# Two of four attention heads' results transposed by 16-bit DMA transposes, and their on-chip places rearranged

## The chip, the cores and the metric

One NeuronCore of a Trainium2 chip runs the whole kernel. The metric is the device time of one execution in microseconds (us), and the time of a kernel is the median of its runs. About 0.2% (some 7 us) is what a measurement of this kernel can tell from no change.

## What is computed

The input is 32 graphs of 512 nodes with 512 features each, and a 512 x 512 adjacency for each. Two pre-normed attention layers follow one another. The reference, cut to what matters here:

```python
h = relu(layernorm(x)); x = x + L0(h, adj)          # one head, attention over the nodes, no projection
h = relu(layernorm(x)); x = x + L1(adj, h)

def gat_layer(x, mask, W, a_src, a_dst, bias, concat):   # L1 calls it twice
    xl = (x @ W).reshape(B, N, H, F)
    asrc = einsum('bnhf,hf->bnh', xl, a_src);  adst = einsum('bnhf,hf->bnh', xl, a_dst)
    e = leaky_relu(asrc[:, :, None, :] + adst[:, None, :, :], 0.2)
    attn = softmax(where(mask[..., None], e, -1e9), axis=1)
    out = einsum('bsdh,bshf->bdhf', attn, xl)
    return (concat over heads, or mean) + bias
# in L1:
h = elu(gat_layer(x, mask, W1, ..., concat=True))    # H = 4 heads of F = 256
h = gat_layer(h, mask, W2, ..., concat=False)        # one head, 1024 -> 512
```

The place of the change is the elu between the two calls of `gat_layer`: the output of each head is 512 nodes x 256 features with the nodes on the partitions, and the product with W2 contracts over the features, so that it needs them on the partitions. Each head's result is therefore transposed.

## The kernel before

The sizes are T = 4 node tiles of P = 128 nodes, KD = 4 blocks of 128 features, H = 4 heads. Everything is float32 but the masks, which are bf16.

**Order of the work.** The function `tile_preln_gat_kernel` (L261) doesn't emit instructions in the order in which it is written. It hands each one to `Plan.op` (L59) as a closure, with the engines that may run it, a cost for each, and the parts of buffers that it reads and writes. `Plan.run` (L87) then drafts a schedule up to six times: a list scheduler (L131) simulates five engines, a chain of transfers (L140, L210 to 215: one at a time, at most eight in flight) and the places of each kind of buffer (`slots`, L317), ranks the work by its latest start and emits the best draft. So the order on each engine, which place a buffer gets, and which of two engines runs an eviction are decided at build time by these costs. On the chip each engine runs its own list strictly in that order.

**One graph**, in the loop at L985: `masks1` and `layer1_project` (W1), `layer2_out` of the graph before, the four heads (`layer1_scores`, then `layer1_head`), `layer0_out` and `layer1_in` of the next graph, `layer0_scores` of the one after, and `layer2_project` (W2). The plan mixes these, so that TensorE has matmuls of neighbouring graphs to run while a chain of another waits.

- `edge_weights` (L583) makes one head's 512 x 512 weights `E`: rows of scores go through DRAM and come back broadcast over the partitions (`in_lines` L548, `row_of` L565, into a `row` place), a largest value is taken (L592), then per tile a leaky relu (L613, ACT), a subtraction (L616, DVE), the mask (L618, POOL) and an exponential (L621, ACT).
- `aggregate` (L624) multiplies `E` by the head's values: for each node tile four matmuls, L631. Each is two TensorE instructions in the trace. Its first matmul also takes the place of the result, so TensorE can't begin before that place is free.
- `layer1_head` (L887) divides by the row's sum and adds the bias (L894, L897, DVE) into `v`, a place of [128, 4, 256] for the whole head; then for each half of the node tiles an exponential of v - 1 (L906, ACT, into the one place `e`) and min/max (L909, DVE). The bias has been raised by 1 at the start (L419), so that `v` holds elu + 1. Eight TensorE transposes (L921, recorded at L485) turn the head over, feature block by feature block, into two PSUM banks; `evict` (L514) takes each bank to `h1T` on ACT (L520) or DVE (L526), subtracting the 1.
- `layer2_project` (L930) multiplies by W2 with `products` (L774), a seven-product scheme on quarters (node half i, contraction half j). Its matmuls are L826, its sums of quarters L807 (DVE) and L808 (POOL); `h1T[0]` (heads 0 and 1) and `h1T[1]` (heads 2 and 3) are the two contraction halves.
- The masks are transposed by DMA already: `transposed_mask` (L669) issues four transfers of [128, 512] bf16 per mask from the SP queue (L673). SP also issues the loads and stores of `x` (L660, L762, L770, L964).

The places that matter here:

```python
        "v": places("v", 2, [P, T, F]),
        "e": places("e", 1, [P, T // 2, F]),
        "row": places("row", 2, [P, N]),
```

All three hold 2 KB per partition in 512 values, `v` twice that.

Of the kernel before, what the change touches and what calls it, by code (L numbers as in the profile page):

```python
# [9 lines left out]
F32 = mybir.dt.float32  # L10
BF16 = mybir.dt.bfloat16
AF = mybir.ActivationFunctionType
ALU = mybir.AluOpType
PSUM = bass.MemoryType.PSUM

P = 128
# [26 lines left out]
class Plan:  # L43
# [87 lines left out]
    def draft(self, rank):  # L131
# [7 lines left out]
        now = {e: [] for e in names}  # L139
        lock, moving, landed = {"DVE": 0.0, "POOL": 0.0}, 0.0, []  # L140
        vacant = {kind: [(0.0, k) for k in range(len(s))] for kind, s in self.slots.items()}
# [22 lines left out]
        while len(draft.order) < len(ops):  # L164
# [42 lines left out]
            if locks and e in lock:  # L207
                at = max(at, lock["POOL" if e == "DVE" else "DVE"])
                lock[e] = at + occupied
            for held in moves:  # L210
                if len(landed) >= self.IN_FLIGHT:
                    at = max(at, landed[-self.IN_FLIGHT])
                moving = max(moving, at) + held
                there += moving - at
                landed.append(at + there)
# [39 lines left out]
def by_dma(n, after=2000.0):  # L255

    return 350.0, after, n / 300.0


@with_exitstack  # L260
def kernel(  # L261
# [51 lines left out]
    def places(kind, n, shape, dtype=F32, pool=big):  # L313
# [14 lines left out]
        "E_one": places("E_one", 2, [P, T, N]),  # L328
        "v": places("v", 2, [P, T, F]),
        "e": places("e", 1, [P, T // 2, F]),  # L330
        "col": places("col", 12, [P, T]),
        "ac": places("ac", 4, [P, 4, T]),
        "row": places("row", 2, [P, N]),
        "r": places("r", 8, [P, 1]),
# [16 lines left out]
    minus_half = const.tile([P, T], F32, name="minus_half")  # L351
    nc.vector.memset(minus_half, -0.5)
    minus_one = const.tile([P, 1], F32, name="minus_one")
    nc.vector.memset(minus_one, -1.0)
# [25 lines left out]
    AHEAD, LATER = 400, 300  # L380
    NEAR0, NEAR2, FAR = False, False, ()

# [3 lines left out]
    def load_constants():  # L386
# [12 lines left out]
        for k in range(KD):  # L399
            for half, q in enumerate(QUARTER[k // (KD // 2)]):  # L400
# [3 lines left out]
                )  # L404
        fetch(HF, lambda: b1_r, rows(b1, HF), W["b1"](1), -LATER)
        fetch(D, lambda: b2_r, rows(b2, D), W["b2"](0), -LATER)
# [4 lines left out]
        for i in range(2):  # L411
# [5 lines left out]

        op(
            "DVE", on_dve(HF), lambda: nc.vector.tensor_scalar(b1_r, b1_r, 1.0, None, op0=ALU.add), W["b1"](1), W["b1"](0),  # L419
            -LATER,  # L420
        )
        return att
# [91 lines left out]
    def evict(src, dst, src_of, dst_of, n, bias=None, psum_half=False):  # L514
# [13 lines left out]
        op(("ACT", "DVE"), (on_act(n, bias is not None), on_dve(n)), (by_act, by_dve), src, dst)  # L528

    def spread(part, col_of, ahead):  # L530

        row = Buffer("acc")
        for t in range(T):
            pe_transpose(
                ahead, row, lambda t=t: row.at[:, node_block(t)], part, lambda t=t: col_of(t).to_broadcast([P, P]), ident, t
            )
        return row
# [7 lines left out]
    def first(ac, n):  # L545
        return lambda: ac.at[:, :n, :].rearrange("p n t -> p (n t)")

    def in_lines(cols_of, part, n):  # L548

        pt, flat_, lines = Buffer("acc"), Buffer("e"), Buffer("lines")  # L550
        m = n * T
        op(
            "PE", on_pe(P, transpose=True),
            lambda: nc.tensor.transpose(pt.at[:m, :P], cols_of(), ident),  # L554
            part + flat_("place"), pt(0), AHEAD,
        )
        evict(pt(0), flat_(0), lambda: pt.at[:m, :P], lambda: flat_.at[:m, 0, :P], P)
        op(
            "SP", by_dma(4 * m * P, 3000.0),
            lambda: nc.sync.dma_start(lines.at[:n].rearrange("n (t p) -> (n t) p", p=P), flat_.at[:m, 0, :P]),  # L560
            flat_(0), lines(0), AHEAD,
        )
        return lines
# [105 lines left out]
    def transposed_mask(m, mT):  # L669
        for t in range(T):  # L670
            op(
                "SP", (2200.0, 3000.0, 600.0),
                lambda t=t: nc.sync.dma_start(mT.at[:, :, node_block(t)], m.at[:, t, :], transpose=True),  # L673
                m(t), mT(t),
            )
# [36 lines left out]
    def layer0_scores(b):  # L712
# [16 lines left out]

        L0[b] = (h0, edge_weights("E_one", scores, ac, in_lines(first(ac, 2), scores, 2) if b else None, 0, m0, m0T, not b or NEAR0))  # L730

# [5 lines left out]
    def layer1_in(b):  # L737
# [5 lines left out]
        for k in range(KD):  # L743
            pt = Buffer("acc")
            for t in range(T):
                pe_transpose(
                    AHEAD, pt, lambda t=t, pt=pt: pt.at[:, node_block(t)], hn(t) + hT("place"),
                    lambda t=t, k=k: hn.at[:, t, node_block(k)], ident, t,
                )
            evict(pt(*ROW), hT((k, 0), (k, 1)), lambda pt=pt: pt.at, lambda k=k: hT.at[:, k, :], N)  # L750
        HT[b] = hT
# [104 lines left out]
    def layer1_project(b):  # L856
# [8 lines left out]
        def dst(i, j, r, c):  # L865
# [4 lines left out]
            lambda i, j: hT.at[:, j * nk : (j + 1) * nk, i * HN : (i + 1) * HN],  # L870
            lambda i, j, g: hT(*((j * nk + 2 * g + k, i) for k in range(2))),
            nk, weights_of("w1", KINDS_1), W1, range(H // 2), lambda w, k, c: w1_s[w][:, k, c, :], dst, xl,
        )

    def layer1_scores(b, h):
# [8 lines left out]
        ac, lines = AC[b]  # L884
        return edge_weights("E", ac(0), ac, lines, 2 * j, m1T, m1, h not in FAR)

    def layer1_head(b, h, E):  # L887

        xl, j = L1[b][h // 2], h % 2
        v = Buffer("v")  # L890
        for t in range(T):
            acc = aggregate(E, t, xl, lambda s: ((j, s),), lambda s: xl_of(xl)[:, s, j, 2:], F + 1, v)
            r = Buffer("r")
            op("DVE", on_dve(8), lambda acc=acc, r=r: nc.vector.reciprocal(r.at, acc.at[:, F : F + 1]), acc(0) + xl(2), r(0))  # L894
            op(
                "DVE", on_dve(F, 1.0, True),
                lambda t=t, acc=acc, r=r: nc.vector.scalar_tensor_tensor(  # L897
                    v.at[:, t, :], acc.at[:, :F], r.at, b1_r[:, h * F : (h + 1) * F], op0=ALU.mult, op1=ALU.add
                ),
                acc(0) + r(0) + W["b1"](0), v(t),  # L900
            )
        for half in range(2):
            ts = slice(half * T // 2, (half + 1) * T // 2)
            parts = v(*range(T)[ts])
            e = Buffer("e")
            op("ACT", on_act(2 * F, 1), lambda e=e, ts=ts: nc.scalar.activation(e.at, v.at[:, ts, :], AF.Exp, bias=minus_one), parts, e(0))  # L906
            op(
                "DVE", on_dve(2 * F),
                lambda e=e, ts=ts: nc.vector.scalar_tensor_tensor(  # L909
                    v.at[:, ts, :], e.at, 1.0, v.at[:, ts, :], op0=ALU.min, op1=ALU.max  # L910
                ),
                parts + e(0), parts, lock=True,
            )
# [3 lines left out]
        nk = F // P  # L917
        for k in range(nk):
            pt = Buffer("acc")
            for t in range(T):  # L920
                pe_transpose(  # L921
                    0, pt, lambda t=t, pt=pt: pt.at[:, node_block(t)], v(t) + h1T("place"), lambda t=t, k=k: v.at[:, t, node_block(k)], ident, t
                )
# [6 lines left out]
    def layer2_project(b):  # L930
# [19 lines left out]
        )  # L950
        L2[b] = (edge_weights("E_one", ac(0), ac, in_lines(first(ac, 2), ac(0), 2) if b < B - 1 else None, 0, m1T, m1, b == B - 1 or NEAR2), xl)

# [84 lines left out]
```

## Time and profile before

| | before |
|---|---|
| median of 3 runs | 3676.41 us (3674.74 to 3678.61) |
| profiled execution: its own time | 3677.66 us |
| its span, first to last instruction | 3675.7 us |
| TensorE (PE) busy | 3598.6 us, 98%, 17620 matmul instructions |
| weight loads (PEld) busy | 3118.9 us, 85% |
| VectorE (DVE) busy | 2953.4 us, 80% |
| ScalarE (ACT) busy | 1873.2 us, 51% |
| GpSimd (POOL) busy | 1456.5 us, 40% |
| DMA | mean 89 GB/s; the SP queue's packets took 26.9% of 16 engines' span |
| granted TensorE clock | 0.994 of full speed |

Engine names are PE, DVE, ACT, POOL and SP; a name with q is the sequencer, and a group such as "L621 ACT ACTIVATE E<-E 128x512" is all instructions of that line, engine, operation and shape, with count, summed busy time and mean duration. Matmuls overlap in the pipeline, so the duration of one is longer than the distance between two starts. A transfer has two times: how long SP is held by issuing it, and how long after that it lands.

### The profile page before, as it was taken

How to read it: one execution, taken by the hardware profiler on the slowest of the kernel's cores; microseconds unless marked ns; L12 is line 12 of the kernel's file. 1: busy time of each engine (PE TensorE's matmuls, PEld its weight loads, DVE VectorE, ACT ScalarE, POOL GpSimd, SP SyncE). 2: the span in 40 equal slices, each digit the busy share in tenths (PEclk: the TensorE clock that was granted, in tenths of full speed). 3: DMA queues.
4: the chain of work that ended last, by engine and by line, in shares of the span. 5: the costliest groups of instructions: out<-in, count | busy, mean ns of one | idle time of the engine just before them, and what ended most of it. 6: DMA issues, size and time to landing. Idle time of an engine off the chain costs nothing.

```text
span 3675.7 us, 51476 instructions
## 1 busy us (share of the span) xinstructions
PE 3598.6 (98%) x17620; PEld 3118.9 (85%) x17620; DVE 2953.4 (80%) x7487; ACT 1873.2 (51%) x3426; POOL 1456.5 (40%) x1269
## 2 busy tenths in 40 slices
PE   5799999999999999999999999999999999999999
PEld 4688888888888888888888888888888888888877
DVE  7888778877788887788777888877887877887755
ACT  2455455555455555555555555554555545555543
POOL 3534334433334343344343344333443433443322
PEclk9899999999999999999999999999999999999999
DMA  6234333343333343323333323433233433333220
GB/s 166 58 92 109 76 90 85 79 109 89 91 85 89 86 110 84 88 82 87 98 99 83 88 89 81 110 87 92 81 92 87 109 78 90 85 82 106 86 65 32
DMA packets 313767, 328.54 MB, mean 89 GB/s; under 512 B 151736, under 2 KB 190368, under 8 KB 313504
## 3 DMA queue, kind: packets, MB, share of 16 engines
q1 hardware_dynamic: 279712, 291.70, 26.9%
q0 software_dynamic: 33792, 33.56, 6.4%
q8 instruction: 138, 2.26, 0.2%
q14 instruction: 125, 1.02, 0.1%
HBM read 257.16 MB, written 68.01 MB: 88 GB/s over the span
## 4 chain that ended last, share of the span: by engine, by line
PE 95%; DVE 2%; ACT 0%; POOL 0%; issue 0%; DVEq 0%
PE acc L631 47%; PE acc L826 42%; PE acc L485 6%; PE acc L554 1%; DVE junk L592 1%; DVE E L616 0%; DVE x L649 0%; DVE E_one L616 0%; DVE st L491 0%; ACT E_one L621 0%; DVE v L897 0%; DVE w L457 0%; POOL E L618 0%; POOL E_one L618 0%; DVE junk L375 0%
## 5 line engine op out<-in xcount | busy, mean ns | idle before, releaser
L631 PE MATMUL acc<-pair,E 128*128 128x257 f32 x4096 | 950.2, 381 | 5.5 <-ACT E L621 5.5
L618 POOL TENSOR_TENSOR E<-E,m 128x512 f32<-128x512 f32 x512 | 596.6, 1189 | 769.6 <-DVE E L616 527.5
L631 PEld LDWEIGHTS acc<-pair,E 128*128 128x128 f32 x4096 | 760.0, 190 | 110.1 <-ACT E L621 7.1
L826 PE MATMUL acc<-w_T,E 128*128 128x257 f32 (+1 forms) x2048 | 517.9, 380 | 0.0
L631 PE MATMUL acc<-h,E_one 128*128 128x256 f32 (+1 forms) x2048 | 479.7, 381 | 4.8 <-ACT E_one L621 4.8
L592 DVE CUSTOM_DVE_ANT_0 junk<-m1T,acc 128x512 bf16<-128x512 bf16 x640 | 436.2, 682 | 29.1 <-ACT acc L580 16.5
L631 PE MATMUL acc<-xl,E_one 128*128 128x257 f32 x1984 | 459.6, 379 | 0.0
L621 ACT ACTIVATE E<-E 128x512 f32<-128x512 f32 x512 | 317.0, 625 | 272.3 <-POOL E L618 266.5
L826 PEld LDWEIGHTS acc<-w_T,E 128*128 128x128 f32 x2048 | 383.4, 190 | 61.5 <-DVE E L807 0.2
L631 PEld LDWEIGHTS acc<-h,E_one 128*128 128x128 f32 x2048 | 381.8, 190 | 61.3 <-ACT E_one L621 5.8
L631 PEld LDWEIGHTS acc<-xl,E_one 128*128 128x128 f32 x1984 | 370.5, 189 | 50.8 <-ACT E_one L621 0.7
L839 DVE TENSOR_TENSOR pair<-acc,pair 128x258 f32<-128x258 f32 (+1 forms) x390 | 164.6, 424 | 300.6 <-PE acc L826 261.1
L613 ACT ACTIVATE E<-row,ac 128x512 f32<-128x512 f32 x512 | 343.7, 708 | 80.9 <-PE acc L631 78.1
L518 ACT COPY pair<-acc 128x258 f32<-128x258 f32 (+1 forms) x486 | 181.4, 374 | 380.2 <-PE acc L826 376.1
L906 ACT ACTIVATE e<-v,minus_one 128x512 f32<-128x512 f32 x256 | 184.8, 722 | 317.8 <-DVE v L897 221.8
L616 DVE TENSOR_TENSOR E<-E,acc 128x512 f32<-128x512 f32 x512 | 324.5, 674 | 3.4 <-PE acc L485 3.2
L618 POOL TENSOR_TENSOR E_one<-E_one,m0T 128x512 f32<-128x512 f32 x128 | 144.8, 1155 | 335.9 <-DVE E_one L616 335.8
L826 PE MATMUL acc<-w,hT 128*128 128x258 f32 x1024 | 268.1, 381 | 0.0
L826 PE MATMUL acc<-w,E 128*128 128x257 f32 (+1 forms) x1024 | 267.6, 381 | 0.0
L909 DVE SCALAR_TENSOR_TENSOR v<-e,v 128x512 f32<-128x512 f32 x256 | 225.6, 881 | 44.0 <-ACT e L906 42.3
L667 POOL DMA_DIRECT2D m<-in_adj_dram x64 | 51.5, 805 | 502.2 <-DVE col L592 465.9
L649 DVE SCALAR_TENSOR_TENSOR x<-acc,r,x 128x256 f32<-128x256 f32 x512 | 239.3, 478 | 13.6 <-PE acc L631 7.3
(108 smaller groups left out, 5899.7 us busy)
## 6 DMA issues: line engine op xcount, KB each, us to landing
row<-lines SPq DMA_DIRECT2D x442, 256.0 KB, 3.5
x<-in_x_dram SPq DMA_DIRECT2D x32, 1024.0 KB
m<-in_adj_dram POOLq DMA_DIRECT2D x64, 512.0 KB, 5.8
spill<-x SPq DMA_DIRECT2D x32, 1024.0 KB, 4.4
x<-spill SPq DMA_DIRECT2D x32, 1024.0 KB, 5.5
out_dram<-x SPq DMA_DIRECT2D x30, 1024.0 KB
m0T<-m SPq DMA_TRANSPOSE x128, 2.5
m1T<-m SPq DMA_TRANSPOSE x128, 2.8
```

The source lines that it names most:

```text
L485: op("PE", on_pe(P, transpose=True), lambda: nc.tensor.transpose(dst_of(), src_of(), identity), src, dst(part), ahead)
L518: nc.scalar.copy(dst_of(), src_of())
L592: lambda t=t: nc.vector.tensor_tensor_reduce(junk, mask_max.at[:, t, :], a_row.at, 1.0, LOWEST, ALU.add, ALU.max, accum_out=amax.at[:, t : ...
L613: lambda t=t: nc.scalar.activation(E.at[:, t, :], c_row.at, AF.Prelu, bias=a_of(t), scale=1.0, alpha=SLOPE),
L616: op("DVE", on_dve(N), lambda t=t: nc.vector.tensor_sub(E.at[:, t, :], E.at[:, t, :], m_row.at), m_row(*ROW) + E(t), E(t))
L618: "POOL", on_pool(N, True), lambda t=t: nc.gpsimd.tensor_add(E.at[:, t, :], E.at[:, t, :], mask.at[:, t, :]),
L621: op("ACT", on_act(N), lambda t=t: nc.scalar.activation(E.at[:, t, :], E.at[:, t, :], AF.Exp), E(t), E(t))
L631: lambda s=s: nc.tensor.matmul(acc.at[:, :n], E.at[:, s, node_block(t)], of(s), start=(s == 0), stop=(s == T - 1)),
L649: lambda acc=acc, r=r, f=f, t=t: nc.vector.scalar_tensor_tensor(X.at[:, t, f], acc.at[:, :HD], r.at, X.at[:, t, f], op0=ALU.mult, op1=ALU. ...
L826: lambda k=k: nc.tensor.matmul(acc.at[:, :width], at[a]()[:, k, node_block(r)], weight_of(w, k, c), start=(first and k == 0), stop=(k == n ...
L906: op("ACT", on_act(2 * F, 1), lambda e=e, ts=ts: nc.scalar.activation(e.at, v.at[:, ts, :], AF.Exp, bias=minus_one), parts, e(0))
L909: lambda e=e, ts=ts: nc.vector.scalar_tensor_tensor(v.at[:, ts, :], e.at, 1.0, v.at[:, ts, :], op0=ALU.min, op1=ALU.max),
```

## The change

In heads 0 and 1 (`TURNED`), the TensorE transposes and the PSUM evictions go. Instead, for each half (two node tiles, 512 float32 values per partition): the elu itself is formed, as max(v, -relu(1 - exp(v))), in two ACT instructions and one on DVE; ACT copies it, seen as 1024 16-bit values, into a `row` place with low and high halves separated; SP issues one transposing DMA of [128, 1024] 16-bit values, eight blocks of 128 x 128, back into the `v` place; and ACT copies from there into `h1T`, interleaving the halves again. Heads 2 and 3 keep the TensorE transposes.

`v` becomes four places of half a head, and the kind `e` is given up: there are three `row` places, which rows of scores, flat lines (`in_lines`), exponentials and the separated halves share. The 1 is added to the bias of heads 2 and 3 only. The planner charges a transposing transfer with its own two-part cost (`by_turning`) and now follows ordinary transfers and transposes in two chained queues. The rest of the diff (finer parts of `hT`; flags that were constant written out) doesn't alter what is run.

```diff
-        lock, moving, landed = {"DVE": 0.0, "POOL": 0.0}, 0.0, []
+        lock, taken, landed = {"DVE": 0.0, "POOL": 0.0}, [0.0, 0.0], []
...
-            for held in moves:
+            if moves:
                 if len(landed) >= self.IN_FLIGHT:
                     at = max(at, landed[-self.IN_FLIGHT])
-                moving = max(moving, at) + held
-                there += moving - at
+                for k, held in enumerate(moves):
+                    taken[k] = max(taken[: k + 1] + [at]) + held
+                there += taken[len(moves) - 1] - at
                 landed.append(at + there)
...
+def by_turning(n):
+    return 1100.0 + n / 1000.0, 800.0, n / 300.0, 1400.0 + n / 180.0
...
-        "v": places("v", 2, [P, T, F]),
-        "e": places("e", 1, [P, T // 2, F]),
+        "v": places("v", 4, [P, 2, F]),
...
-        "row": places("row", 2, [P, N]),
+        "row": places("row", 3, [P, N]),
...
+    TURNED = (0, 1)
...
+    def turned(values_of, src, place, results_of, dst):
+        e = Buffer("row")
+        op(
+            "ACT", (1040.0, 1100.0),
+            lambda: nc.scalar.copy(
+                e.at.bitcast(U16).rearrange("p (b f) -> p b f", b=2), values_of().bitcast(U16).rearrange("p (f b) -> p b f", b=2)
+            ),
+            src + place, e(0),
+        )
+        op(
+            "SP", by_turning(4 * P * N),
+            lambda: nc.sync.dma_start(
+                values_of().bitcast(U16).rearrange("p (c n) -> p c n", n=P), e.at.bitcast(U16), transpose=True
+            ),
+            e(0), src,
+        )
+        def pair():
+            out = results_of()
+            k, t = out.shape[1], out.shape[2]
+            nc.scalar.copy(
+                out.bitcast(U16).rearrange("p k t (n b) -> p k t n b", b=2),
+                values_of().bitcast(U16).rearrange("p (b t k n) -> p k t n b", b=2, k=k, t=t),
+            )
+        op("ACT", (1160.0, 1220.0), pair, src, dst)
...
-                "SP", (2200.0, 3000.0, 600.0),
+                "SP", by_turning(2 * P * N),
...
-        v = Buffer("v")
+        vs = [Buffer("v"), Buffer("v")]
         for t in range(T):
+            v, i = vs[2 * t // T], t % (T // 2)
...
+        for half in range(2):
+            v, e = vs[half], Buffer("row")
+            parts = v(*range(T // 2))
+            values = lambda v=v: v.at.rearrange("p t f -> p (t f)")
+            if h in TURNED:
+                op("ACT", on_act(2 * F), lambda e=e, values=values: nc.scalar.activation(e.at, values(), AF.Exp), parts, e(0))
+                op(
+                    "ACT", on_act(2 * F, 1),
+                    lambda e=e: nc.scalar.activation(e.at, e.at, AF.Relu, bias=one, scale=-1.0), e(0), e(0),
+                )
+                op(
+                    "DVE", on_dve(2 * F),
+                    lambda e=e, values=values: nc.vector.scalar_tensor_tensor(
+                        values(), e.at, -1.0, values(), op0=ALU.mult, op1=ALU.max
+                    ),
+                    parts + e(0), parts, lock=True,
+                )
+                turned(
+                    values, parts, h1T("place"),
+                    lambda half=half: h1T_of(h1T)[:, j * nk : (j + 1) * nk, half * HN : (half + 1) * HN].rearrange(
+                        "p k (t n) -> p k t n", n=P
+                    ),
+                    h1T(*((j * nk + k, half) for k in range(nk))),
+                )
+                continue
...
-        for k in range(nk):
+        for k in () if h in TURNED else range(nk):
             pt = Buffer("acc")
```

## The prediction, made before the result was known

> **What bounds the kernel now.** I read the page's busy times first, then PE's waits, then the PE timeline of one graph.
>
> ```profile
> PE 3598.6 (98%) x17620; PEld 3118.9 (85%) x17620; DVE 2953.4 (80%) x7487; ACT 1873.2 (51%) x3426; POOL 1456.5 (40%) x1269
> ...
> PE 95%; DVE 2%; ACT 0%; POOL 0%; issue 0%; DVEq 0%
> ```
>
> The second line is the chain that ended last: 95% of the span is PE behind PE. A busy PE alone would not prove a full one, so here are PE's waits between 160 and 3520 us, and the busy times of 500 us in the middle.
>
> ```profile
> PE acc L485 <- DVE v L909: 1.3, 1, 1.3
> PE acc L485 <- DVE col L599: 0.7, 1, 0.7
> PE acc L631 <- ACT E_one L621: 0.3, 1, 0.3
> ...
> 1500.00:2000.00 500.00, 500.00 (x2458) 433.93 (x2458) 403.44 (x1017) 257.63 (x477) 195.19 (x172) 1.00 0.33 90
> ```
>
> In 3360 us PE waits 2.3 us. Everything else is hidden, and a PE instruction removed there is gained whole unless a new wait appears. How much one is worth is seen in the PE timeline (start, length, count):
>
> ```profile
> 1505.02 1.47 PE L826 MATMUL acc<-w,pair 128*128 128x257 f32 x6
> 1506.33 1.90 PE L826 MATMUL acc<-w_T,E 128*128 128x257 f32 x8
> 1508.07 1.90 PE L826 MATMUL acc<-w,pair 128*128 128x257 f32 x8
> ...
> 1613.81 0.60 PE L485 MATMUL acc<-ident,v 128*128 128x128 f32 x4
> 1614.25 1.89 PE L631 MATMUL acc<-h,E_one 128*128 128x256 f32 x8
> ```
>
> Eight matmuls take 1508.07 - 1506.33 = 1.74 us, 0.2175 each; four transposes take 1614.25 - 1613.81 = 0.44 us, 0.109 each. One graph repeats every 111.83 us (the same long L826 piece of the chain stands at 396.01 and 507.85). Pricing all PE instructions so gives 3587 us, and PE's idle 77 us lie almost wholly in the first 130 us (the constants, on DVE) and the last 200.
>
> **What the Trainium skill says.** (1) "TensorE: Matmul & The Clock Gate", Part 4, gives about 275 ns for a transpose in a kernel. The trace's mean is 273, but that is one's length in the pipeline; the distance, 109 ns, is what a removed one gives back. The measurement decides. (2) "DMA: Bandwidth & Descriptors", DMA Transpose (X-bar), takes 2-byte types only, so float32 must be split into halves and joined again. The mask transposes, bf16, agree. It also forbids two transposing streams at once; here all are SP's, so no wait is added. (3) The same page, HWDGE ordering, says an engine consumes descriptors in ring order: a transpose issued behind a 1 MB load on SP's queue stands behind its data. No row shows the two together. (4) "ScalarE: Activation LUTs", What ACT_TABLE_LOAD costs: 186 ns + 0.833 ns an element, 93 more for a pointer bias, back-to-back overlapping by 93. The trace agrees within a few per cent: 587 ns for the copy L580 of 512 (613 by the page), and in ACT's timeline an L613 starts 0.51 us after a 0.58 us L580.
>
> **The change, part by part.** The rows that give durations:
>
> ```profile
> L906 ACT ACTIVATE e<-v,minus_one 128x512 f32<-128x512 f32 x256 | 184.8, 722 | 317.8 <-DVE v L897 221.8 <-DVE r L894 94.6 <-issue 1.2
> ...
> L485 PE MATMUL acc<-ident,v 128*128 128x128 f32 x1024 | 153.7, 273 | 2.7 <-DVE v L909 2.7
> ...
> L520 ACT ACTIVATE pair<-acc,minus_one 128x512 f32<-128x512 f32 x161 | 105.9, 678 | 98.9 <-PE acc L485 98.9
> ...
> L526 DVE TENSOR_SCALAR pair<-acc 128x512 f32<-128x512 f32 x95 | 64.6, 680 | 7.4 <-PE acc L485 7.4
> ...
> L673 SPq DMA_TRANSPOSE m1T<-m x128: 1188/1201/2461, 82.8 to 3567.0; - x128
> ...
> DMA to landing us min/median/max: 2.4/2.5/4.2
> ```
>
> *Removed on PE.* Of the 1024 transposes of `v`, 512 go: 16 a graph. 16 x 0.109 = 1.74 us a graph, x 32 = **-55.7 us**, all on the path.
>
> *Other engines, from the order of the changed program.* ACT gains 128 relus of about 0.70 (as L520), 128 separating and 128 joining copies of 1024 elements; it loses 96 L520 (0.68), 29 hT (0.59) and 147 projection evictions (0.37), and half its L906 become plain exponentials (0.72 to 0.63). The copies are new: 587 + 512 x 0.833 = 1.01 us from L580, 1.04 by the page. Below, 0.6 if 16-bit values went at double pace; above, 2.0 if the strided 2-byte side halved it. I take 1.04. Sum +90 + 266 - 137 - 12 = +207 us: ACT at about 2080 of 3622, 57%. DVE gives up 32 L526 (22 us) and 55 sums of quarters (70) and takes the evictions that ACT lost (82): about level, 81%. POOL takes the sums, +83 us, 43%. None is a bound; the free time of ACT and DVE hides it. The bias split and the finer `hT` parts cost nothing measurable; they hide behind the start's loads.
>
> *The transfers.* Per graph four transposes of 256 KB. The nearest row is the masks' 128 KB: 1.2 us on SP, then 2.5 to land. With twice the blocks it is at least the same and at most twice: 1.2 to 2.4 on SP, 2.5 to 5.0 landing; I take 1.6 and 3.7. SP gets 4 x 1.6 = 6.4 us a graph, and in the new order they stand behind the store of `out` and the load of `x`, ahead of the spill (L762) and load-back (L770), which wait for later work anyway. While two mask transposes are issued back to back (1559 to 1562.5 us) DMA is 0.54 busy, so four of twice the size at that rate (4 x 2.5 x 0.54 = 5.4 us of 110) add some 5% of the DMA's time.
>
> *The added wait.* A `v` place is taken by the first matmul of `aggregate`, so TensorE itself waits for it, with all PE work queued behind. Heads 2 and 3 take the places that heads 0 and 1 leave after the joining copy. In the new PE order, from the last matmul of a half of head 0 to the first that takes its place again, there are 14.3 to 15.2 us of PE work at the cadences above. One half's own chain: 1.1 (reciprocal, two L897) + 0.63 + 0.70 + 0.88 (L909) + 1.04 + 1.6 + 3.7 + 1.04 = 10.7 us, some 0.4 more for signals. That leaves 3 us, but ACT is in order: between the first half's exponential and its joining copy stand 16 other ACT instructions (7 exponentials of `E` or `v`, 7 relus and leaky relus, 2 copies). At the distances of ACT's timeline, 0.53, 0.61 and 0.95, and with the exponential and the joining copy themselves, they come to 11.5 us; begun 1.0 after the last matmul, they end at 12.5. So ACT, not the chain, sets the margin: 1.8 us on the tightest place. The transfer has 6.6 us between the separating and the joining copy. With my values (5.3) it fits; with the upper ends (7.4) it is 0.8 late, inside the margin; behind a 1 MB load still moving (spill<-x lands in 4.4) it can be later. The second consumer, W2, has more room: 23 us of PE work from head 1's last matmul to the first L826.
>
> *Shared rows.* Three places serve what two `row` and one `e` served, with 4 more short holders a graph. A late row stops ACT (L580 waited 36.3 us for rows in all), which has 43% spare; I cost it at nothing, at most 0.3 us a graph if that cover goes.
>
> *Ends.* In the first and last graph PE has no spare matmuls to put into these chains: I allow 4 us, between -5 and +12. For occasional misses of the tight place I allow 0.1 us a graph, 3 us; bounds 0 to 3.4 a graph (below). Sum against the profiled execution: 3677.7 - 55.7 + 4 + 3 = 3629.0. The median of runs lies 1.3 lower: **3628 us**.
>
> **The rivals.**
>
> *A. Part of the gain is lost at the places.* If the 16-bit copies take their upper end, 2.0 us, the three in ACT's stretch add 2.9 us, 1.1 more than the margin, and PE waits that much a graph: 3676.4 - 55.7 + 4 + 32 x 1.1 = 3660. For it speaks how little margin there is; against it, that ACT's durations in the trace follow the number of elements, and that PE's waits for all places together are 2.3 us before.
>
> *B. Slower: the transposes land behind the load of `x`.* SP's order puts the store of `out` and the 1 MB load just ahead of the first of the four. If the ring makes it wait for the load's 4.4 us, and it takes 2.4 + 5.0 itself, the joining copy comes 11.8 us after the separating one where 6.6 are covered: 5.2 late, less the margin of 1.8, and PE stands 3.4 us at the place, while ACT holds the exponentials of head 3 behind the joining copy. It decides from 1.74 us of wait a graph, a transfer of 10.1 us. At 3.4: 3676.4 + 32 x (3.4 - 1.74) + 4 = 3733 us. Against it: only the first of the four can meet the load, and the load takes its full time only if it starts as late.
>
> *C. The change doesn't give the PE time back, since another engine takes over.* DVE at 81% is nearest; between 500 and 3500 us it had 18% free with PE waiting for it 2 us. It would have to wait on POOL and ACT at the wrong times, 1.74 us a graph: no change, 3676. The shares speak against it.
>
> **Chances.** Forecast (3612 to 3640) 0.62; A (3640 to 3669) 0.15; C or about level (3669 to 3684) 0.06; B (above) 0.17. Faster by over 0.2% 0.77, within 0.2% 0.06 (0.2% is about what a measurement of this kernel can tell from no change), slower 0.17. The range runs from the full gain with better ends, 3612, through A to level, 3676; B is left out.
>
> **What would show it.** Right: 17108 PE instructions, a graph every 110.1 us, PE's waits in the middle still a few us; the new SP row near 1.6 with landing near 3.7; the two ACT copies near 1.04; ACT near 57%. Rival A or B: PE acc (the L631 of before) waits for ACT's joining copy in most graphs, and that copy waits for the DMA of `v` (B) or not (A). I am wrong if the transfers land in over 5 us, if the copies cost over 1.3 us, or if PE waits for rows.

## The result, and the profile after

The changed kernel takes **3658.15 us** (median of 5 runs, 3656.49 to 3661.75), the kernel before 3677.87 on the same chip: a ratio of 0.995, 95% interval 0.9936 to 0.9965. That is faster by 19.7 us, where 48 were forecast. The time lies inside the range, but under half of the predicted gain came.

First the page of the changed kernel: the engines' busy times, and the chain that ended last.

```profile
PE 3557.8 (97%) x17108; PEld 3059.5 (84%) x17108; DVE 2966.4 (81%) x7521; ACT 2075.1 (57%) x3595; POOL 1560.7 (43%) x1324
...
PE 78%; DVE 11%; POOL 2%; DMA 2%; ACT 2%; issue 1%; SPq 1%; DVEq 0%; ACTq 0%; POOLq 0%
```

The first line is what the prediction asked for: 17108 PE instructions, ACT at 57%, DVE at 81%, POOL at 43%. The second line is not. Before, 95% of the chain was PE behind PE; now DVE holds 11%. So PE stands somewhere. Here are PE's waits between 160 and 3500 us of the changed kernel (total us, times, longest), and then 500 us in the middle:

```profile
PE acc L497 <- DVE col L641: 16.2, 27, 1.5
PE acc L673 <- ACT E_one L663: 1.8, 5, 0.6
PE acc L868 <- DVE pair L881: 0.9, 1, 0.9
```

```profile
1500.00:2000.00 500.00, 497.52 (x2404) 428.72 (x2403) 406.86 (x1022) 286.81 (x505) 217.82 (x185) 1.00 0.39 101
```

PE was busy in every one of these 500 us before, and is idle for 2.5 of them now. None of the waits is for a place of `v` or for a joining copy, which rivals A and B and most of the prediction were about. PE waits for `col`, a head's maxima: L641 (L599 before) is a DVE instruction on 128x4 values, and L497 with `ident,col` is the spread that lays them along a row. The lines are those of the changed kernel from here on.

The new instructions themselves, from the groups of the changed kernel, and the view of the transposing transfer's line (durations in ns, min/median/max; then issue to landing in us):

```profile
L565 ACT COPY pair<-v 128x1024 uint16<-128x1024 uint16 x128 | 147.3, 1150 | 0.6 <-DMA v<-row 0.6
L549 ACT COPY row<-v 128x1024 uint16<-128x1024 uint16 x128 | 132.5, 1035 | 12.2 <-DVE v L962 9.1 <-issue 1.2
```

```profile
L556 SPq DMA_TRANSPOSE v<-row x128: 1232/1232/1516, 133.0 to 3595.0; - x128
...
DMA to landing us min/median/max: 2.7/2.7/2.7
```

The separating copy (L549) took 1.035 us and the joining one (L565) 1.150, where 1.04 was taken for each; the issue held SP for 1.23 us (1.6 taken). The 2.7 us run from the start of the issue to landing, so SP's time is part of them. The view knows the landing of only 15 of the 128 transfers. By the trace's completion records, of which some are missing, the median of all 128 is 2.7 us as well, but 14 took 4 us or more (at most 5.8), and ten of these were issued 2 to 3.3 us after the load of `x`. Only once in the kernel did a joining copy wait for its transfer (SP's issue, then ACT's copy):

```profile
1253.59 1.23 SPq L556 DMA_TRANSPOSE v<-row  x1
1258.84 1.16 ACT L565 COPY pair<-v 128x1024 uint16<-128x1024 uint16 x1 [0.57 <-DMA v<-row]
```

This transfer took 5.2 us, cost ACT 0.57 us, and no wait of PE names it.

**What one stand looks like.** Three timelines of the changed kernel around 1558 us (start, length; in brackets the idle time before it and its releaser), PE, DVE, then POOL:

```profile
1555.54 2.76 PE L673 MATMUL acc<-xl,E_one 128*128 128x257 f32 x12
1559.50 0.65 PE L497 MATMUL acc<-ident,col 128*128 128x128 f32 x4 [1.20 <-DVE col L641]
```

```profile
1558.11 0.15 DVE L639 TENSOR_TENSOR col<-ac,col 128x4 f32<-128x4 f32 x1
1558.18 0.48 DVE L691 SCALAR_TENSOR_TENSOR x<-acc,r,x 128x256 f32<-128x256 f32 x1
1558.58 0.87 DVE L641 SCALAR_TENSOR_TENSOR col<-col 128x4 f32<-128x4 f32 x1
1559.37 0.15 DVE L685 RECIPROCAL r<-acc 128x1 f32<-128x1 f32 x1
```

```profile
1558.27 1.16 POOL L660 TENSOR_TENSOR E_one<-E_one,m 128x512 f32<-128x512 f32 x1 [1.65 <-DVE col L639]
```

L641 has four elements a partition; its sister L639 takes 0.15 us. Here it takes 0.87, and ends at 1559.45, 0.02 after GpSimd's addition of the mask does (1558.27 + 1.16 = 1559.43). PE starts 0.05 later. Of the 1.20 us that PE waits here, the collision makes 0.72; the rest is a chain that was late already. The pattern holds throughout: in the changed kernel 21 of the 192 L641 and 20 of the 192 L639 took over 0.3 us, and each of these 41 ended 16 to 24 ns after a GpSimd instruction did.

The larger L691 reads one of its two big inputs from PSUM; GpSimd starts 0.09 us into it, and neither is stretched. All of this is what the Trainium skill describes on "SBUF — State Buffer", Who interferes with whom (and above it, SBUF: two separate sides): DVE and GpSimd share one pair of ports as an exclusive lock; a DVE instruction with two SBUF inputs and a GpSimd instruction that reads SBUF don't share it, the later one waits for the whole of the earlier. The kernel's planner knows that rule (`lock=True` on an operation), but the two 128x4 operations L639 and L641 don't carry the mark.

**Collisions alone are not new.** In the kernel before the same instruction (L599 there) was stretched as well, as its mean in the groups of before shows:

```profile
L599 DVE SCALAR_TENSOR_TENSOR col<-col 128x4 f32<-128x4 f32 x192 | 48.9, 255 | 3.0
```

255 ns there, 229 in the changed kernel. In the kernel before, PE had other work queued ahead of the spread (0.7 us of waits for `col` in all); in the changed order, the spread stands next. So the theory to test has two halves: the collision, and an order in which nothing covers it.

### The profile page after: what moved, and what is told of

Its sections match the earlier page's. It is cut to its first block, busy times and chain, and to the rows that moved or that the text cites. A ratio compares the mean times of both kernels' runs of the same rounds, so it can differ in the third digit from the quotient of the medians.

```text
span 3656.0 us, 51114 instructions
## 1 busy us (share of the span) xinstructions
PE 3557.8 (97%) x17108; PEld 3059.5 (84%) x17108; DVE 2966.4 (81%) x7521; ACT 2075.1 (57%) x3595; POOL 1560.7 (43%) x1324
## 4 chain that ended last, share of the span: by engine, by line
PE 78%; DVE 11%; POOL 2%; DMA 2%; ACT 2%; issue 1%; SPq 1%; DVEq 0%; ACTq 0%; POOLq 0%
PE acc L673 37%; PE acc L868 36%; PE acc L497 4%; DVE junk L634 4%; POOL E_one L660 2%; DVE E_one L658 2%; DVE x L691 1%; DVE E L658 1%; DMA row<-lines 1%; SPq L715 1%; DMA m0T<-m 1%; DVE pair L881 0%; ACT E L655 0%; PE acc L596 0%; DVE col L639 0%
## 5 line engine op out<-in xcount | busy, mean ns | idle before, releaser
L673 PE MATMUL acc<-pair,E 128*128 128x257 f32 x4096 | 924.4, 380 | 4.6 <-ACT E L663 4.6
L660 POOL TENSOR_TENSOR E<-E,m 128x512 f32<-128x512 f32 x512 | 618.6, 1238 | 344.7 <-DVE E L658 312.8
L673 PE MATMUL acc<-h,E_one 128*128 128x257 f32 (+1 forms) x2048 | 497.2, 382 | 8.6 <-ACT E_one L663 4.8
L655 ACT ACTIVATE E<-row,ac 128x512 f32<-128x512 f32 x512 | 334.6, 708 | 12.6 <-DMA row<-lines 12.3
L658 DVE TENSOR_TENSOR E<-E,acc 128x512 f32<-128x512 f32 x512 | 332.4, 674 | 2.9 <-PE acc L497 2.1
L530 ACT COPY pair<-acc 128x258 f32<-128x258 f32 (+1 forms) x339 | 126.5, 374 | 309.4 <-PE acc L868 307.3
L530 ACT COPY xl<-acc 128x257 f32<-128x257 f32 x219 | 82.0, 374 | 345.9 <-PE acc L868 345.7
L941 DVE SCALAR_TENSOR_TENSOR v<-acc,r,b_r 128x256 f32<-128x256 f32 x512 | 242.5, 478 | 8.5 <-DVE r L938 0.7
L868 PE MATMUL acc<-w,pair 128*128 128x257 f32 x1024 | 244.3, 379 | 0.0
```

The source lines that it names most:

```text
L530: nc.scalar.copy(dst_of(), src_of())
L655: lambda t=t: nc.scalar.activation(E.at[:, t, :], c_row.at, AF.Prelu, bias=a_of(t), scale=1.0, alpha=SLOPE),
L658: op("DVE", on_dve(N), lambda t=t: nc.vector.tensor_sub(E.at[:, t, :], E.at[:, t, :], m_row.at), m_row(*ROW) + E(t), E(t))
L660: "POOL", on_pool(N, True), lambda t=t: nc.gpsimd.tensor_add(E.at[:, t, :], E.at[:, t, :], mask.at[:, t, :]),
L673: lambda s=s: nc.tensor.matmul(acc.at[:, :n], E.at[:, s, node_block(t)], of(s), start=(s == 0), stop=(s == T - 1)),
L868: lambda k=k: nc.tensor.matmul(acc.at[:, :width], at[a]()[:, k, node_block(r)], weight_of(w, k, c), start=(first and k == 0), stop=(k == n ...
```

## The measure used below

PE's idle time in the trace understates the loss, because short pauses lie inside modelled durations. I added up, from 500 to 3020 us of PE's timeline, the distance between the starts of successive pieces less what their count should take (0.109 us a transpose, 0.2172 a matmul), and took off the same sum of the kernel before, which holds the artefacts of cutting the timeline. Divided by the 22.5 graphs of that stretch it is the **stand per graph**: 26.1 / 22.5 = 1.16 us in the changed kernel. A time follows: 3677.5, less 55.7 where the 512 transposes are gone, plus 32 stands. The changed kernel: 3677.5 - 55.7 + 37.1 = 3659, measured 3658.

| kernel | PE instructions | stand per graph, us | worked out, us | measured, us |
|---|---|---|---|---|
| before | 17620 | 0 (reference) | 3677 | 3677 |
| changed | 17108 | 1.16 | 3659 | 3658 |
| none_turned | 17620 | 2.89 | 3770 | 3764 |
| masks_old_price | 17108 | 0.52 | 3638 | 3646 |
| before_unturned | 17108 | 0.05 | 3623 | 3629 |
| small_locked | 17108 | -0.03 | 3621 | 3626 |
| one_input | 17108 | 0.49 | 3637 | 3639 |
| none_one_input | 17620 | 0.71 | 3700 | 3690 |
| signal_61 | 17108 | 1.60 | 3673 | 3672 |
| before_prices | 17620 | 0.46 | 3692 | 3689 |
| none_locked | 17620 | 1.57 | 3728 | 3727 |
| before_locked | 17620 | 0.81 | 3703 | 3704 |
| before_places | 17620 | 0.51 | 3694 | 3692 |
| all_locked | 17108 | 0.15 | 3627 | 3629 |

Two numbers a kernel, its PE work and its stand, give every time within 11 us, eight of the thirteen within about 3. Nothing is needed for the transfers, the copies or ACT's extra work. The sum says how long PE stood, not why; that is what the experiments are for. A second reading agrees within 0.2 us a graph for every kernel: the distance from one graph to the next in the trace (first transposes of `h`, mean over 21 graphs), 111.83 us before and 111.27 in the changed kernel.

## The experiments

The theories: **collision**, as above. **Prices**: the planner's new prices for the mask transposes make a worse order. **Lost cover**: the removed transposes had covered waits that now show. **Turned path**: the copies and transfers themselves hold something up. **Re-planning**: any change of the plan moves the time so much, with no one cause.

### none_turned: the changed kernel with no head turned

```diff
-    TURNED = (0, 1)
+    TURNED = ()
```

> The changed kernel with no head turned by transfers (TURNED empty): its planner and its places, but all four heads transposed on TensorE. Prices theory (the mask transposes' new, lower price on SP took slack out of the plan, and TensorE now stands at the spread of a head's maxima behind late score rows): the loss of about 1.1 us a graph is there without any turning, 3677 + 35 = 3712 us, with TensorE waiting for DVE's maxima in most graphs. Turned-path theory (the copies and transfers of the turned heads disturb ACT, SP and DVE): like the kernel before, 3677 us. Lost-cover theory (1.74 us less TensorE work a graph leaves the score chain uncovered): 3677 us too.

Measured 3763.92 us, ratio 1.0234 (1.0219 to 1.0249): far above every theory. PE's waits of this kernel:

```profile
PE acc L497 <- DVE col L641: 40.5, 60, 1.4
PE acc L497 <- DVE v L981: 13.1, 14, 1.0
```

The same wait, two and a half times as large, in a kernel without a single turned head. So the loss doesn't need the copies and transfers, and in the changed kernel no wait of PE names them: the turned path falls. Measured against this kernel, turning gains 106 us, almost twice the PE work that it removes; that is the difference of two orders, not a price of turning.

### masks_old_price: the mask transposes planned at their old price

```diff
-                "SP", by_turning(2 * P * N),
+                "SP", (2200.0, 3000.0, 600.0),
```

> The changed kernel with one edit: the mask transposes are planned at their old price (2.2 us on SP, 3.0 after, 0.6 moving) in place of the new one. Nothing else is edited; the plan's order changes. Prices theory: the waits for DVE's maxima go, 3658 - 33 = 3625 us. Turned-path and lost-cover theories: unchanged within some 8 us, 3650 to 3666 us.

Measured 3645.76 us, 0.9914 (0.9899 to 0.9929): between the two expectations. The waits for `col` are gone, but in their place PE waits for `v` of DVE (4.5 us, 16 times). The price matters through the order it makes, but the old price doesn't bring the rest of the gain.

### before_unturned: the PE work alone

The kernel before, with heads 0 and 1 not transposed at all: the copy to `h1T` takes `v` as it lies. It leaves out these two heads' transposition.

```diff
+            if h < 2:
+                evict(
+                    v(*ROW) + h1T("place"), h1T((j * nk + k, 0), (j * nk + k, 1)), lambda k=k: v.at[:, :, node_block(k)],
...
+                )
+                continue
```

> The kernel before, with the transposes of heads 0 and 1 left out and nothing in their place: the evictions copy the untransposed values from v to the same place (so the output of layer 1 is computed from untransposed values in these two heads). Its planner, prices and places are those of before. It shows what the removed TensorE work is worth with no turned path at all. Prices theory and turned-path theory: the whole 55.7 us, 3620 to 3625 us, no waits in the middle. Lost-cover theory: the score chain is uncovered here too, 3650 us or more.

Measured 3628.91 us, 0.9869 (0.9855 to 0.9884): 48.5 us, of the 55.7 that the removed transposes were priced at, and 4 us above the expectation. PE is full in its middle (busy in all of the 500 us from 1500), and the 3650 or more that lost cover asked for is far off: lost cover falls. A graph repeats here every 110.26 us, where the full gain would give 110.09, so by estimate some 5 of the missing 7 us are pauses too short to show as waits.

### small_locked: the two small operations marked for the planner

```diff
-        op("DVE", on_dve(T), lambda: nc.vector.tensor_add(z.at, ac.at[:, k + 1, :], amax.at), scores + amax(*ROW), z(0))
+        op("DVE", on_dve(T), lambda: nc.vector.tensor_add(z.at, ac.at[:, k + 1, :], amax.at), scores + amax(*ROW), z(0), lock=True)
...
-            z(0), m(0),
+            z(0), m(0), lock=True,
```

> The changed kernel with one edit: the two small DVE instructions between a head's maxima and their spread are planned apart from GpSimd's work (lock), as one of them took 0.87 us beside GpSimd where 0.15 is usual. Contention theory (that instruction is what TensorE waits for): most of the waits go, 3635 us. Prices theory: its 0.7 us is only part of a late chain; 3645 to 3658 us. Others: 3658 us.

Measured **3626.29 us**, 0.9861 (0.9845 to 0.9878): the fastest kernel of the study, 31.9 us under the changed one. Its waits of PE and a stretch of its middle:

```profile
PE acc L868 <- DVE pair L881: 0.5, 1, 0.5
PE acc L673 <- DVE E L658: 0.4, 1, 0.4
PE acc L673 <- DVE x L691: 0.2, 1, 0.2
```

```profile
1500.00:2000.00 500.00, 500.00 (x2420) 433.77 (x2419) 413.00 (x1045) 291.92 (x520) 212.52 (x186) 1.00 0.41 104
```

PE is full again. But how? The small operations are still stretched in this kernel:

```profile
L641 DVE SCALAR_TENSOR_TENSOR col<-col 128x4 f32<-128x4 f32 x192 | 56.8, 296 | 0.1
```

296 ns, more than the 229 of the changed kernel (its sister L639 194, against 221). The mark did not take the collisions away; it gave an order in which PE has something else to do. This run can't tell a cured collision from a lucky new order. The next one can.

### one_input and none_one_input: the collision removed, the order kept

The two operations keep their place in the plan, but each reads one SBUF tensor instead of two. They leave the other score and the slope out of the number that is subtracted before the exponential (it cancels in the softmax). The order on every engine is that of the changed kernel, or of none_turned: in the traces the two kernels of each pair run the same sequence on PE, DVE, ACT, POOL and SP, without one difference but the two replaced operations.

```diff
+        def alone(dst, src):
+            nc.vector.tensor_reduce(dst, src.rearrange("p (t o) -> p t o", o=1), mybir.AxisListType.X, ALU.max)
...
-        op("DVE", on_dve(T), lambda: nc.vector.tensor_add(z.at, ac.at[:, k + 1, :], amax.at), scores + amax(*ROW), z(0))
+        op("DVE", on_dve(T), lambda: alone(z.at, amax.at), scores + amax(*ROW), z(0))
...
-            "DVE", on_dve(T), lambda: nc.vector.scalar_tensor_tensor(m.at, z.at, SLOPE, z.at, op0=ALU.mult, op1=ALU.max),
+            "DVE", on_dve(T), lambda: alone(m.at, z.at),
```

> The changed kernel, same order of instructions on every engine, but the two small DVE instructions between a head's maxima and their spread read one SBUF operand each instead of two (the maxima are copied twice; the other score and the slope are left out of the number that softmax subtracts, which cancels in the softmax). Collision theory (with two SBUF operands each of them waits for the GpSimd instruction that is running, and TensorE waits for them): their duration falls to about 0.15 us everywhere, TensorE's waits for them go, 3618 to 3630 us. Re-planning theory (the locked version was only a luckier plan): the plan is unchanged, so 3658 us.

> The same edit in the version with no head turned (3764 us), again with an unchanged order. Collision theory: most of the 86 us above the kernel before go, 3680 to 3695 us. Prices theory (rows of scores come late because the mask transposes are planned too cheaply): at most a quarter goes, 3740 us or more.

Measured 3639.28 us (0.9894, 0.9878 to 0.9909) and 3689.72 us (1.0034, 1.0021 to 1.0046): 18.9 us less than the changed kernel, and 74.2 less than none_turned (of the 86.5 that none_turned was above the kernel before), with every instruction in its old place. The group in one_input:

```profile
L627 DVE TENSOR_REDUCE col<-col 128x4 f32<-128x4 f32 x384 | 56.1, 146 | 0.1
```

146 ns on the mean, as an undisturbed one, and none of the 384 took over 157. The stand of 1559.50 in the changed kernel, which lasted 1.20 us, is here:

```profile
1554.00 0.65 PE L497 MATMUL acc<-ident,col 128*128 128x128 f32 x4 [0.38 <-DVE col L627]
```

This shows the collision as a cause: re-planning can't explain a gain in a plan that did not change. It also gives its size. 18.9 us is about half of what the stand costs (37 worked out); one_input still stands 0.49 us a graph. Between 160 and 3500 us its PE waits for `col` 4.4 us (9 times, without any collision of L627) and for E_one 2.7 us (6 times). Here is one stand of each, first E_one in PE's and ACT's timelines:

```profile
1545.01 0.59 PE L673 MATMUL acc<-h,E_one 128*128 128x256 f32 x2
1546.75 0.48 PE L673 MATMUL acc<-h,E_one 128*128 128x257 f32 x1 [1.14 <-ACT E_one L663]
```

```profile
1544.84 1.33 ACT L655 ACTIVATE E<-row,ac 128x512 f32<-128x512 f32 x2 [1.42 <-DMA row<-lines]
1546.08 0.61 ACT L663 ACTIVATE E_one<-E_one 128x512 f32<-128x512 f32 x1
```

Here PE waits for an exponential, the exponential stands behind two L655 on ACT, and the first of them waited 1.42 us for a row's transfer. For `col`, on ACT, DVE and PE:

```profile
2210.24 0.59 ACT L622 COPY acc<-row 128x512 f32<-128x512 f32 x1 [1.25 <-DMA row<-lines]
2210.86 1.28 DVE L658 TENSOR_TENSOR E_one<-E_one,acc 128x512 f32<-128x512 f32 x2 [1.61 <-ACT acc L622]
2217.18 0.65 PE L497 MATMUL acc<-ident,col 128*128 128x128 f32 x4 [0.79 <-DVE col L627]
```

ACT's copy waits for a row, DVE waits for the copy, and from there DVE works without a pause up to the L627 that PE needs. Both stands begin with a late row. Late rows are not a cost by themselves: in small_locked ACT waits for rows more (56.4 us in all against 29.8 in the changed kernel), and PE stands nowhere. A kernel in one_input's order with rows landing sooner was not tried on the chip, so the share of the rows in the remaining 0.49 us stays open.

### signal_61 and before_prices: other plans

signal_61 is the changed kernel with the planner's allowance for a signal between engines a nanosecond higher, which makes another order of the same work; before_prices is the kernel before with the new prices and lanes of the planner and its own places.

```diff
-    SIGNAL = 60.0
+    SIGNAL = 61.0
```

```diff
-        lock, moving, landed = {"DVE": 0.0, "POOL": 0.0}, 0.0, []
+        lock, taken, landed = {"DVE": 0.0, "POOL": 0.0}, [0.0, 0.0], []
...
-                "SP", (2200.0, 3000.0, 600.0),
+                "SP", by_turning(2 * P * N),
```

> A control: the changed kernel with the planner's signal time 61 in place of 60 ns, which means nothing on the chip but makes another plan. If any other plan is as good as the locked one: 3620 to 3630 us. If the plan's blindness to collisions is what costs: it depends on where the two small instructions fall this time, 3630 to 3700 us, and TensorE's waits for DVE's maxima go with the time.

> The kernel before with the planner of the changed one (transposes' new price, two chained queues), its own places and no turning. Prices theory: 3700 us or more, as in the version with no head turned. Places theory (it is the shared and halved places that make that version slow): 3677 us. Collision theory: no fixed number; the excess over 3677 comes as waits for the two small instructions.

Measured 3672.01 us (0.9986, 0.9979 to 0.9993) and 3689.01 us (1.0033, 1.0022 to 1.0045). In signal_61 PE waits for `col` 15.5 us, as in the changed kernel, and for E_one 4.5. So the changed kernel's 3658 is itself one draw among orders that a nanosecond in the plan tells apart, and with the new prices the kernel before is 11.5 us slower, part of it again in waits for `col` (5.6 us).

### none_locked, before_locked, before_places, all_locked: is the mark a cure?

The mark of small_locked on none_turned and on the kernel before; none_turned with the planner's old prices and lane; and, in the changed kernel, the mark on the layernorm's two small operations (L505, L512) as well. The edit of before_places against none_turned, and what all_locked adds to small_locked:

```diff
-        lock, taken, landed = {"DVE": 0.0, "POOL": 0.0}, [0.0, 0.0], []
+        lock, moving, landed = {"DVE": 0.0, "POOL": 0.0}, 0.0, []
...
-                "SP", by_turning(2 * P * N),
+                "SP", (2200.0, 3000.0, 600.0),
```

```diff
-        op("DVE", on_dve(T), lambda: nc.vector.tensor_scalar(ve.at, mv.at[:, :, 1], EPS, None, op0=ALU.add), mv(*ROW), ve(0))
+        op("DVE", on_dve(T), lambda: nc.vector.tensor_scalar(ve.at, mv.at[:, :, 1], EPS, None, op0=ALU.add), mv(*ROW), ve(0), lock=True)
...
-            mv(*ROW) + rstd(0), nmr(0),
+            mv(*ROW) + rstd(0), nmr(0), lock=True,
```

> The changed kernel with no head turned (all four by TensorE transposes), and the two 128x4 instructions of a head's maxima told to the planner as contending with GpSimd. Collision theory: PE's waits for col go as they did with the lock alone; what is left over the locked changed kernel's 3626.3 us is the PE work of 512 transposes, 32 x 16 x 0.109 = 55.7 us, less the few us that turning costs at the ends: 3675 to 3685 us, and level with the kernel before. Rival (the shared places or the 16-bit layout cost time that only turning covers): near the 3763.9 us of the same kernel without the lock, at least 3720.

> The kernel before with the same two instructions told to the planner as contending with GpSimd. Control. Collision theory: the kernel before waits for col 0.7 us in its whole middle, so there is nothing to cure: 3670 to 3683 us. Rival (the mark simply finds the planner a better order, whatever the kernel): some 30 us or more faster, 3645 us or less.

> The changed kernel with no head turned and with the planner's old view of the mask transposes (old price, one lane), so that against the kernel before only the places and the layout of heads differ. If the shared and halved places by themselves move the work into collisions: 3720 us or more, as with the new prices (3763.9). If places and prices only do so together, or by accident of the order: 3670 to 3700 us.

> The changed kernel with the two 128x4 instructions of the maxima and the two of the layernorm (mean 634 and 696 ns in the changed kernel, 250 and 277 before) told to the planner as contending with GpSimd. Collision theory: with the first two alone PE waited 1.1 us in the middle, so the layernorm's two have nothing left to give there: 3620 to 3632 us. Rival (collisions of the layernorm also cost PE time): under 3618 us.

- **none_locked** 3727.27 us (1.0137, 1.0122 to 1.0153): my expectation failed. The waits for `col` did go, but PE waits for `v` (9.9 us), `h` (8.4) and E_one (4.6) instead. The number is where the rival put it, but the rival's reason (places and layout cost time) is spoken against by none_one_input and before_places, with the same places at 3690 and 3692.
- **before_locked** 3704.41 us (1.0075, 1.0063 to 1.0088): neither theory. The kernel before gets 28 us *slower* by the mark. Its small operations are less stretched than ever (L599 165 ns), and yet PE stands 0.81 us a graph at the transposes of `h`, which come as ACT ends:

```profile
PE acc L485 <- ACT h L508: 6.5, 28, 0.2
```

- **before_places** 3691.80 us (1.0041, 1.0028 to 1.0053), inside the expectation for places and prices that do harm only together: with the new places and halves alone the kernel is some 15 us slower, not the 86 of none_turned. It is one order again, so this is no price of the places.
- **all_locked** 3629.16 us (0.9869, 0.9856 to 0.9883), as the collision theory has it: in this order the layernorm's mark gains nothing more.

So the collision is a real cost in the changed kernel's order, but the mark is no cure in general: it brought 32 and 37 us in two kernels and took 28 in a third. What decides is which order the plan falls into, and where that order leaves PE without cover.

## Why the prediction was wrong, step by step

- **PE's removed work: right.** Where PE does not stand, the kernel takes 3626.3 (small_locked), 1.7 from the forecast; that is 51.2 us under before, for 55.7 less an allowance of 4 at the ends. A graph repeats there every 110.09 us; 110.1 was forecast.
- **The new copies and the transfers: near enough, with one slip.** Copies 1.035 and 1.150 for 1.04; SP 1.23 for 1.6; landing 2.7 for 3.7. The slip: the view counts landing from the start of the issue, while the chain of the prediction added both times, 1.6 + 3.7 = 5.3 us, where 2.7 passed. That made the tight place look tighter than it was. The price that the prediction took from the Trainium skill, "ScalarE: Activation LUTs", What ACT_TABLE_LOAD costs (1.04 us by the page), holds for the separating copy; the joining one is 11% above it.
- **The tight place of `v`: never tight.** The prediction spent most of its care here, and no PE wait names it. Rivals A and B rested on it. Transfers that landed late did occur, most of them soon after the load of `x` as B had it; two took over 5 us by the completion records, which the prediction had named as a sign of being wrong, but no PE wait came of it. The measured time is next to A's 3660, but by another mechanism, so that is luck.
- **Shares of the engines: right** (57, 81 and 43%), **and the conclusion from them wrong.** "None is a bound; the free time of ACT and DVE hides it" is the step that failed, and with it the term "for occasional misses of the tight place I allow 0.1 us a graph, 3 us". The measured term is 1.16 us a graph, 37 us, and most of it lies at another spot: of PE's waits in the middle, 16.2 us are at the spread of a head's maxima, and no other wait there has over 1.8. The collisions are shown for 18.9 of the 37 us (one_input); the rest is not cleared up. A busy share of 81% says nothing about the one 128x4 instruction that PE needs next, when it is locked out for 0.7 us.
- **Rival C came nearest in kind.** I had written that DVE "would have to wait on POOL and ACT at the wrong times, 1.74 us a graph", and gave it 0.06, because before PE waited for DVE 2 us in 3000. PE stood two thirds of that, and the collisions with POOL are shown for half of what it stood. The evidence I set against it was a property of the old order; the change makes a new one.
- **Shared rows at nothing, at most 0.3 us a graph:** open. No run measured them alone. ACT waited for rows less than before in all (29.8 us, against 38.7), but two of the stands that one_input keeps begin with a late row, and how much of the changed kernel's 1.16 us needs both a late row and a collision isn't known.
- **"A graph every 110.1 us":** 111.83 - 1.74 + 1.16 gives 111.25, and the trace has 111.27.

What stays open: why the orders with and without turned heads fall where they do. Ten of the thirteen kernels of the table below the first row stand between 0.4 and 2.9 us a graph, at different spots (`col`, `v`, `h`, `xl`, E_one), and I found no rule that tells which from the diff.

## What to carry to other kernels

When a program writes the order, a change re-draws the whole order, and the kernel before is one draw: its lack of waits is not a stock that the new one inherits. Look for short instructions that the bounding engine waits for directly, find which of them can be locked out by a neighbour without the planner's knowledge, and allow for that in the sum; here the stand was 37 us against a gain of 56, and 19 of the 37 are shown to be collisions. To tell a cause from a lucky order, keep the order and change only the suspected instruction.

## What the runs showed of the hardware that was not expected

A DVE instruction on 128x4 values with two SBUF inputs, 0.15 us alone, took 0.87 us beside a 1.16 us GpSimd addition and ended within 0.02 us of it; with one SBUF input in the same place, the mean is 146 ns. One input alone is no safeguard for every operation, though: the layernorm's L505, a tensor_scalar on 128x4 values with one SBUF input, took 0.16 us at the least and over 0.3 in 48 of 64 cases in the changed kernel, and each of the 48 ended 22 to 28 ns after a GpSimd instruction did. And a 256 KB transposing transfer holds SP about as long as a 128 KB one (1.23 us; 1.20 for the masks in the same trace) and lands about as soon where the view knows the landing (2.7 us in 15 of 128, 2.6 in 17 of 256).
